# Graph sums join Strassen's scheme in two GRU gates, and three buffers are halved to make room

## The chip, the cores and the metric

The kernel runs on one core of a Trainium2 chip. A core has five engines that run side by side: TensorE (PE in the profile; its weight loads are shown apart, as PEld), VectorE (DVE), ScalarE (ACT), GpSimd (POOL) and SyncE (SP), which here only issues DMAs. The metric is the device time of one execution in microseconds (us), as the median over runs.

## What is computed

The layer works on 32 graphs of 512 nodes with 256 features each, in float32:

```python
h = relu(layernorm(x))                              # x: (32, 512, 256)
c = relu(bn1(conv1x1(h)))
x_conv = relu(bn2(conv17(c)) + h)                   # 17 taps along the nodes
s = h @ w_se.T + b_se
A = exp(-|s_n - s_m|^2) * adj
x_nmp = A @ relu(h @ w_msg.T + b_msg)               # the graph sums
gi = concat(x_conv, x_nmp) @ w_ih.T + b_ih          # (.., 768): parts r, z, n
gh = h @ w_hh.T + b_hh
r = sigmoid(gi_r + gh_r); z = sigmoid(gi_z + gh_z)
out = x + (1 - z) * tanh(gi_n + r * gh_n) + z * h
```

## The kernel before

**Layout.** Features stand on the 128 partitions (two halves of 128, the `i` or `o` of the code) and the 512 nodes of a batch along the free dimension. One batch is one graph.

**The streams.** The program is written as five Python generators, "streams": `begins` (normalise and transpose a batch), `rows` (the 1x1 convolution), `conv` (the 17-tap convolution), `graphs` (messages, the exponential, the mask, the graph sums) and `gates` (the GRU). A small planner at the end of the kernel keeps estimated times of every engine and tile. At each step it continues the stream whose clock is least among those not held, and it writes the instructions in that order, once for all. After each step `fill()` gives DVE background work: normalisation, the convolution's operands and the sums below. So the order on each engine is fixed when the kernel is built, and any edit shifts it everywhere after.

**The convolution** is done in seven groups along the nodes of all batches, with a nested scheme of 5 x 5 = 25 products a group. Its operands are made on DVE: `operands(g)` calls `fives` on h1, the stored result of the 1x1 convolution, in 6 phases for the outer operand x1 (two buffers, each about 6.6 KB a partition), and again on each x1 in 2 phases for the inner operands x2. `fives` makes the five combinations with twelve DVE instructions at the outer level. Operands are made at most a few products ahead.

**The input.** `fetch(b)` loads x of batch b into `x_sb` (two buffers). `norm` normalises it in place. From batch TURNED = 8 on `begin(b)` stores it to DRAM, reads it back in 32 x 32 blocks, transposes those on DVE and stores the result as HD[b]; it then has the input of batch b + 2 loaded. Before batch 8 TensorE transposes. In the early part a pool `prep` holds the weights in preparation; `late_pools()` closes it and opens `late` in its place, where all that the gates need stands.

**The gates.** `gates(b)` runs `unit(o)` for both output halves. Batches 1 to 30 are "fast" (FIRST_FAST = 1, PLAIN = 1): for the reset gate r and the update gate z together, the product of the weights (2 x 2 blocks: gate by input half) with the data (2 x 2 blocks: input half by node half, HALF = 256) is done with Strassen's scheme in Winograd's form: seven products of 256 columns in place of eight. `weight_sums()` makes the weights' combinations once (`wsum`), `data_sums(b)` those of the data for each batch on DVE (`tsum`: t13 of 512 elements, t2 and t4 of 256 each). `term(...)` writes one of the seven products for each of its sources. Before the change these are h (`hTb`, with `whh`) and x_conv (`xconv`, with the first half of `wih`). The third source, the graph sums (`xnb`, with the second half of `wih`), is added in the plain way, two matmuls of 512 columns a gate, by the calls

```python
yield from products(ps_r, o, 0, (2,), reset, clear=False)
yield from products(ps_z, o, 1, (2,), update, clear=False)
```

The order in a fast unit is: first r term; a copy of it to `ps_z` on ScalarE; products of the new gate of the unit before (`some_new`); three terms; the fifth product copied out (`fifth`) and added on DVE to r's and z's other half (`spread`), with further products between; the last r term, r's graph sums, `reset()` (tanh on ScalarE); the new gate's hidden products (`hidden`), where they were not written earlier; the last z term, z's graph sums, `update()`. The result `r` has two buffers, `fifth` one tile of its own.

**Loads.** SP's queue issues all loads in order, `load_sums(b, d)` those of the graph sums in halves (`xnb`, two buffers of one half each), the second pair only after the first is used. POOL's queue issues the stores.

Of the kernel before, what the change touches and what calls it, by code (L numbers as in the profile page):

```python
# [13 lines left out]
P = 128  # L14
# [17 lines left out]
G = 4  # L32
# [18 lines left out]
def kernel(  # L51
# [266 lines left out]
    def fetch(b, xs=None):  # L318
        XS[b] = front.tile([P, NT, D], F32, name="x_sb", bufs=2) if xs is None else xs
        step = NT // 2 if b == 0 else NT  # L320
        for c in range(0, NT, step):
            sp.dma_start(
                XS[b][:, c : c + step], x[b].rearrange("(c p) d -> p c d", p=P)[:, c : c + step]
            )
# [48 lines left out]
    def load_sums(b, d):  # L373
        if b < B and (b, d) not in XN:
            settle_stores()
            XN[b, d] = late.tile([P, N], F32, name="xnb", bufs=2)
            sp.dma_start(XN[b, d], ND_[b, d])
            XN_AT[b] = max(XN_AT.get(b, 0.0), done(XN[b, d]))

    fetch(0)  # L380
# [6 lines left out]
    prep_ctx = ExitStack()  # L387
    prep = pool_of(prep_ctx, "prep", 1)
# [216 lines left out]

    def phases(name, n, rv, bufs):

        t = cv.tile([P, n * RV], F32, name=name, bufs=bufs)
        return t[:, : n * rv].rearrange("p (q e) -> p q e", e=rv)

    def operands(g):

        rv = sizes(g)[3]
        h = h1[:, : Q * rv].rearrange("p (q e) -> p q e", q=Q)
        for x1 in fives(h, 6, rv, lambda: phases("x1", 6, rv, 2), again=True):
            yield None
            if x1 is not None:
                yield from fives(x1, 2, rv, lambda: phases("x2", 2, rv, 6))
# [298 lines left out]
    def convolution():  # L917
# [28 lines left out]
        for g in range(NG):  # L946
# [9 lines left out]
            for n in range(25):  # L956
# [6 lines left out]
                if late is None and len(WS) >= 25 and prep.over() <= now + 1.0:  # L963
                    late_pools()
# [47 lines left out]
    def late_pools():  # L1012
        nonlocal late, wih, whh, wsum, tsum
        prep_ctx.close()
        late = pool_of(ctx, "late", 1)
        late.born = prep.over()
        whh = late.tile([P, ND, 3 * D], F32, name="whh")
        wih = late.tile([P, 2 * ND, 3 * D], F32, name="wih")
        sp.dma_start(whh, w_hh)
        sp.dma_start(wih, w_ih)  # L1020
        wsum = late.tile([P, 2, 3, D], F32, name="wsum")
        tsum = [
            [late.tile([P, n, HALF], F32, name=f"t{k}_{j}") for j, n in enumerate((2, 1, 1))]
            for k in range(2)
        ]
# [3 lines left out]
    def weight_sums():  # L1029


        for k, w in enumerate((whh, wih)):
            a11, a12 = w[:, 0, :D], w[:, 1, :D]
            a21, a22 = w[:, 0, D : 2 * D], w[:, 1, D : 2 * D]
            s1, s2, s4 = (wsum[:, k, j, :] for j in range(3))
            dve.tensor_tensor(s1, a21, a22, op=ALU.add)
            dve.tensor_tensor(s2, s1, a11, op=ALU.subtract)
            dve.tensor_tensor(s4, a12, s2, op=ALU.subtract)
            dve.tensor_tensor(a21, a11, a21, op=ALU.subtract)
# [6 lines left out]
    def data_sums(b):  # L1046


        step = T_STEP.get(b, 0)
        if step == 6 or b >= B - PLAIN or sums_free[step > 3] != b:  # L1050
            return
        n, k = divmod(step, 2)
        if (RES if k else HB_AT).get(b, 1e9) > now:
            return
        t = XC[b] if k else HB[b]
        t13, t2, t4 = tsum[k]
        if n == 0:
            dve.tensor_tensor(
                t13, t[:, :, HALF:], t[:, 0, :].rearrange("p (h n) -> p h n", h=2),
                op=ALU.subtract,  # L1060
            )
        elif n == 1:
            dve.tensor_tensor(t2[:, 0], t[:, 1, HALF:], t13[:, 0], op=ALU.subtract)
        else:
            dve.tensor_tensor(t4[:, 0], t[:, 1, :HALF], t2[:, 0], op=ALU.subtract)
        T_STEP[b] = step + 1
        if k == 1:
            T_AT[b, n] = dve.free + 0.3
# [95 lines left out]
    def begin(b):  # L1164
# [4 lines left out]
        if b >= TURNED:  # L1169
# [19 lines left out]
            if b + 2 < B:  # L1189
                later(now + 2.0, lambda: load(b + 2))  # L1190
# [6 lines left out]
        for d in range(ND):  # L1197
            yield gps.free("ps_g")
            norm_t(b, d)
            if d == ND - 1:  # L1200
                begun, turning = b + 1, False
                if b < 2 or b >= G:
                    load(b + (G if b < 2 else 2))
            yield now
# [53 lines left out]
    def gates(b):  # L1258
# [8 lines left out]
        if not NEW:  # L1267
            load_sums(b, 0)
            load_sums(b, 1)
# [7 lines left out]
        def products(ps, o, g, ks, then=None, of=None, clear=True):  # L1277
# [4 lines left out]
            for k in ks:  # L1282
# [9 lines left out]
                if k == 2 and o == ND - 1 and g == 2:  # L1292
                    for d in range(ND):
                        later(now + 2.0, lambda d=d: load_sums(b + 1, d))
# [57 lines left out]
        if b == B - PLAIN:  # L1352
            for w, at in ((whh, w_hh), (wih, w_ih)):
                sp.dma_start(w[:, 0, D : 2 * D], at[:, 0, D : 2 * D])
        def some_new(n):
# [9 lines left out]
            while NEW and n > 0:  # L1365
                NEW.pop(0)()
                n -= 1
                if last and len(NEW) == 2:
                    for d in range(ND):
                        later(now + 0.5, lambda d=d: load_sums(NEW_B[0] + 1, d))  # L1370
# [7 lines left out]
        def unit(o):  # L1378
            r = z = None

            def reset():
                nonlocal r
                if is_last(o):
                    load_res(b, o)
                if OPEN > 1:
                    settle()
                r = late.tile([P, N], F32, name="r", bufs=2)
                act.activation(r, ps_r, AF.Tanh, bias=brz[:, o : o + 1], scale=0.5)
# [41 lines left out]
            if fast:  # L1430
# [9 lines left out]
                sources = ((whh, hT), (wih, XC[b]))  # L1440

                def term(ps, weight, data, begin=False, end=False):
                    for k, (w, t) in enumerate(sources):
                        matmul(
                            ps, weight(k, w), data(k, t),
                            start=(begin and k == 0), stop=(end and k == 1), skip_group_check=True,
# [29 lines left out]
                term(ps_r[:, lo], given(0, 0), part_of(0, lo), begin=True)  # L1476
                if UPDATED[0] < UPDATED[1]:
                    yield now + 0.5
                    if UPDATED[0] < UPDATED[1]:
                        settle()  # L1480
                ps_z = acc.tile([P, N], F32, name="ps_acc")
# [4 lines left out]
                if o == 0:  # L1486
                    for d in range(ND):
                        load_sums(b, d)
                    x_in.extend([XC[b][:, i, :] for i in range(ND)] + [XN[b, d] for d in range(ND)])
                    yield lambda: (b, 1) in T_AT  # L1490
                    yield T_AT[b, 1]
# [4 lines left out]
                fifth = late.tile([P, HALF], F32, name="fifth")  # L1496
# [15 lines left out]
                term(ps_r[:, hi], summed_w(2), part_of(1, hi))  # L1512
                yield XN_AT[b]
                yield from products(ps_r, o, 0, (2,), reset, clear=False)
# [9 lines left out]
                if o == 0:  # L1524
                    yield lambda: (b, 2) in T_AT
                    yield T_AT[b, 2]
                yield z_at
                term(ps_z[:, lo], given(1, 1), summed_t(3))
                if o == ND - 1:
                    sums_free[1] = b + 1  # L1530
                yield now
                UPDATED[1] += 1
                yield from products(ps_z, o, 1, (2,), update, clear=False)
                if o == 0:
                    load_gates(b + 1)

# [16 lines left out]
            if not fast:  # L1553
# [3 lines left out]
                if o == 0:  # L1557
# [4 lines left out]
                    x_in.extend([XC[b][:, i, :] for i in range(ND)] + [XN[b, d] for d in range(ND)])  # L1562
# [265 lines left out]
```

## Time and profile before

| what | value |
|---|---|
| median of 3 runs | 2047.43 us (2046.34 to 2051.44) |
| the profiled execution: its own time | 2048.43 us |
| its span, from the first to the last instruction | 2046.7 us |
| VectorE busy | 1440.9 us, 70% |
| ScalarE busy | 878.0 us, 43% |
| DMA | 185 GB/s on average |
| mean granted TensorE clock | 0.991 of full speed |

The numbers of the profile come from one execution and stand beside its own time. A group of the profile is written as line, engine, operation, output<-inputs, shape and count, then the busy time in us and the mean time of one in ns, then the engine's idle time just before and what ended it. Most instructions pass through helpers, so their line is the helper's (L241 for DVE and ScalarE, L259 for matmuls) and they are told apart by their tiles. A float32 matmul appears as two MATMUL instructions with two weight loads. The drawn ends of matmuls overlap the next one, so their cost is read from start to start.

### The profile page before, as it was taken

How to read it: one execution, taken by the hardware profiler on the slowest of the kernel's cores; microseconds unless marked ns; L12 is line 12 of the kernel's file. 1: busy time of each engine (PE TensorE's matmuls, PEld its weight loads, DVE VectorE, ACT ScalarE, POOL GpSimd, SP SyncE). 2: the span in 40 equal slices, each digit the busy share in tenths (PEclk: the TensorE clock that was granted, in tenths of full speed). 3: DMA queues.
4: the chain of work that ended last, by engine and by line, in shares of the span. 5: the costliest groups of instructions: out<-in, count | busy, mean ns of one | idle time of the engine just before them, and what ended most of it. 6: DMA issues, size and time to landing. Idle time of an engine off the chain costs nothing. (4 is left out here: it accounts for less than half of the span.)

```text
span 2046.7 us, 27748 instructions
## 1 busy us (share of the span) xinstructions
PE 2002.3 (98%) x9347; PEld 1382.9 (68%) x9347; DVE 1440.9 (70%) x2686; ACT 878.0 (43%) x1755; POOL 448.2 (22%) x578
## 2 busy tenths in 40 slices
PE   8999999999999999999999999999999999999998
PEld 4777666666776657776677675667766676675664
DVE  5779787978887368885787774678975678763433
ACT  5554563344534353433453334444244533334221
POOL 2100021231221232122232212241212311113232
PEclk9999999999999999999999999999999999999999
DMA  7455587798897779887887788797985978746564
GB/s 260 171 183 176 204 255 216 185 257 201 224 211 208 175 176 228 191 211 173 203 213 180 187 201 184 165 199 214 221 204 136 200 193 180 161 102 125 88 98 42
DMA packets 581230, 378.75 MB, mean 185 GB/s; under 512 B 457648, under 2 KB 475344, under 8 KB 579952
## 3 DMA queue, kind: packets, MB, share of 16 engines
q1 hardware_dynamic: 419616, 279.02, 49.3%
q0 software_dynamic: 153184, 84.70, 24.0%
q10 hardware_dynamic: 8288, 13.24, 1.8%
q8 instruction: 75, 1.23, 0.2%
q14 instruction: 67, 0.55, 0.1%
HBM read 278.81 MB, written 114.56 MB: 192 GB/s over the span
## 5 line engine op out<-in xcount | busy, mean ns | idle before, releaser
L228 POOL DMA_DIRECT2D out_dram<-o_sb x252 | 275.9, 1728 | 612.7 <-DVE o_sb L241 540.5
L259 PE MATMUL ps_acc<-xnb,wih 128*128 128x512 f32 (+1 forms) x772 | 366.5, 591 | 0.8 <-DVE ps_acc L241 0.7
L259 PEld LDWEIGHTS ps_c<-xd,w 128*128 128x128 f32 x2304 | 285.8, 190 | 50.3 <-ACT ps_c L241 32.4
L259 PEld LDWEIGHTS ps_c<-x,w 128*128 128x128 f32 x2032 | 260.3, 194 | 65.0 <-issue 39.2
L259 PE MATMUL ps_c<-xd,w 128*128 128x135 f32 (+1 forms) x2304 | 290.9, 279 | 1.3 <-ACT ps_c L241 1.1
L259 PE MATMUL ps_c<-x,w 128*128 128x135 f32 (+2 forms) x2032 | 268.6, 281 | 7.2 <-ACT z L241 5.1
L259 PE MATMUL ps_g<-at,msg 128*128 128x512 f32 x512 | 227.4, 593 | 2.1 <-DVE shift L241 1.2
L259 PE MATMUL ps_acc<-hTb,whh 128*128 128x512 f32 (+2 forms) x532 | 213.1, 497 | 5.6 <-ACT r L241 5.6
L259 PE MATMUL ps_acc<-xconv,wih 128*128 128x512 f32 (+2 forms) x532 | 209.1, 495 | 1.8 <-DVE ps_acc L241 1.0
L259 PEld LDWEIGHTS ps_acc<-xnb,wih 128*128 128x128 f32 x772 | 140.4, 190 | 95.8 <-issue 85.8
L241 DVE TENSOR_TENSOR ps_acc<-ps_acc,fifth 128x256 f32<-128x256 f32 x120 | 51.2, 427 | 204.6 <-PE ps_acc L259 188.1
L259 PEld LDWEIGHTS ps_g<-at,msg 128*128 128x128 f32 x512 | 95.6, 190 | 110.4 <-issue 103.1
L259 PEld LDWEIGHTS ps_acc<-hTb,whh 128*128 128x128 f32 x532 | 94.9, 190 | 68.6 <-issue 51.6
L241 DVE SCALAR_TENSOR_TENSOR x<-x,x 128x544 f32<-128x544 f32 (+5 forms) x161 | 137.8, 856 | 3.8
L241 DVE TENSOR_TENSOR msg<-ps_g,bmsg 128x256 f32<-128x256 f32 x128 | 53.3, 418 | 119.9 <-PE ps_g L259 119.7
L259 PEld LDWEIGHTS ps_acc<-xconv,wih 128*128 128x128 f32 x532 | 98.0, 190 | 50.0 <-issue 38.8
L241 DVE TENSOR_TENSOR x<-x 128x272 f32<-128x272 f32 (+5 forms) x280 | 127.8, 497 | 0.4
L259 PE MATMUL ps_g<-wmsg,hTg 128*128 128x259 f32 x496 | 125.1, 382 | 0.0
L259 PE MATMUL ps_acc<-t,wsum 128*128 128x256 f32 x480 | 123.5, 379 | 0.8 <-DVE wsum L241 0.8
L259 PE MATMUL ps_g<-hT,w 128*128 128x512 f32 (+8 forms) x296 | 120.5, 553 | 3.5 <-DMA hT<-hd 3.4
L241 ACT ACTIVATE h<-ps_g,bn_shift,bn_scale 128x252 f32<-128x252 f32 (+8 forms) x212 | 86.6, 483 | 62.9 <-PE ps_g L259 60.1
L259 PEld LDWEIGHTS ps_acc<-t,wsum 128*128 128x128 f32 x480 | 90.0, 190 | 31.3 <-issue 18.7
(147 smaller groups left out, 2984.0 us busy)
## 6 DMA issues: line engine op xcount, KB each, us to landing
w<-wd SPq DMA_DIRECT2D x414, 256.0 KB, 3.8
m_sb<-in_adj_dram SPq DMA_DIRECT2D x384, 64.0 KB, 3.9
hT<-hd SPq DMA_DIRECT2D x33, 512.0 KB, 4.5
hd<-hT POOLq DMA_DIRECT2D x32, 512.0 KB, 5.6
hTb<-hd SPq DMA_DIRECT2D x32, 512.0 KB, 5.4
xnb<-nd SPq DMA_DIRECT2D x64, 256.0 KB, 3.5
out_dram<-o_sb POOLq DMA_DIRECT2D x252, 64.0 KB, 4.7
hTg<-hd SPq DMA_DIRECT2D x31, 512.0 KB, 4.2
```

The lines of the kernel that those rows point to most:

```text
L228: self.engine.dma_start(dst, src, **more)
L241: getattr(self.engine, op)(*tiles, **more)
L259: nc.tensor.matmul(ps, lhsT, rhs, **more)
```

## The change

1. The graph sums become a third source of `term`. `wsum` and `tsum` get a third part; `weight_sums` and `data_sums` make it; the plain products of the graph sums in r and z go. `data_sums` now walks two lists, one for h and x_conv, one for the graph sums, a step of each at a call. `reset()` and `update()` follow the last term directly.
2. The graph sums of a batch are one tile of both halves with two buffers, so that they can be loaded a batch ahead. The first r term is split: its part with the graph sums waits for their load.
3. The fifth product is put into the first half of `r`, which is therefore allotted earlier (`make_r`).
4. The outer operand x1 has one buffer from group 1 on: `fives_alone` makes each of the five combinations from the one before, in place. In group 0 the old function is used, with buffers from two pools.
5. The input has one buffer. Odd batches below 8 use one in `prep`; from batch 8 on the load of b + 1 starts when b is turned. `late_pools()` also waits for eight batches begun and 25 operands.

```diff
     def fetch(b, xs=None):
-        XS[b] = front.tile([P, NT, D], F32, name="x_sb", bufs=2) if xs is None else xs
+        if xs is None:
+            pool_ = prep if b % 2 and b < TURNED else front
+            xs = pool_.tile([P, NT, D], F32, name="x_sb" if pool_ is front else "x_odd", bufs=1)
+        XS[b] = xs
...
+            XN[b] = late.tile([P, ND, N], F32, name="xnb", bufs=2)
+            for d in range(ND):
+                sp.dma_start(XN[b][:, d, :], ND_[b, d])
...
+        for steps in (
+            ((minus, 3, 1),),
+            ((minus, 2, 0), (less2, None, 3), (minus, None, 1)),
+            ((minus, 3, 1), (less2, None, 4), (minus, None, 2)),
+            ((minus, 2, 1), (less2, None, 3), (minus, None, 2)),
+            ((minus, 3, 2), (less2, 1, None)),
+        ):
+            for k, (op, a, b) in enumerate(steps):
+                op(a, b)
+                yield t if k == len(steps) - 1 else None
...
-        for x1 in fives(h, 6, rv, lambda: phases("x1", 6, rv, 2), again=True):
+        if g == 0:
+            more = iter([cv, prep] * 2)
+            firsts = fives(h, 6, rv, lambda: x1_of(next(more), rv), again=True)
+        else:
+            firsts = fives_alone(h, 6, rv, x1_of(cv, rv))
+        for x1 in firsts:
...
-                if late is None and len(WS) >= 25 and prep.over() <= now + 1.0:
+                if late is None and len(WS) >= 25 and len(X2) >= 25 and begun >= TURNED and prep.over() <= now + 1.0:
                     late_pools()
...
-            if b + 2 < B:
-                later(now + 2.0, lambda: load(b + 2))
+            if b + 1 < B:
+                later(now + 0.3, lambda: load(b + 1))
...
-                sources = ((whh, hT), (wih, XC[b]))
+                if o == 0:
+                    load_sums(b)
+                sources = ((whh, hT), (wih[:, :ND], XC[b]), (wih[:, ND:], XN[b]))
...
                 ps_r = acc.tile([P, N], F32, name="ps_acc")
-                term(ps_r[:, lo], given(0, 0), part_of(0, lo), begin=True)
+                term(ps_r[:, lo], given(0, 0), part_of(0, lo), begin=True, of=(0, 1))
...
+                if o == 0:
+                    yield XN_AT[b]
+                term(ps_r[:, lo], given(0, 0), part_of(0, lo), of=(2,))
...
-                fifth = late.tile([P, HALF], F32, name="fifth")
+                make_r()
+                fifth = r[:, :HALF]
                 act.activation(fifth, ps_r[:, hi], AF.Copy)
...
-                term(ps_r[:, hi], summed_w(2), part_of(1, hi))
-                yield XN_AT[b]
-                yield from products(ps_r, o, 0, (2,), reset, clear=False)
+                term(ps_r[:, hi], summed_w(2), part_of(1, hi), end=True)
+                reset()
+                yield now
...
-                term(ps_z[:, lo], given(1, 1), summed_t(3))
+                term(ps_z[:, lo], given(1, 1), summed_t(3), end=True)
                 if o == ND - 1:
                     sums_free[1] = b + 1
+                UPDATED[1] += 1
+                update()
                 yield now
-                UPDATED[1] += 1
-                yield from products(ps_z, o, 1, (2,), update, clear=False)
```

In `fives_alone` an operation that reads phase 3 or later is written twice, once for five phases and once for the sixth; `minus` subtracts, `less2` takes twice its first from its second, and None stands for the buffer itself. The load of the sums moves from the end of a batch's new-gate products (there for the next batch) to the same place for the batch after that.

## The prediction

> **What bounds the kernel now.** I read the page's busy times first, then the same by stage, then what TensorE waits for, then TensorE's order of work where nothing else runs. The busy times:
>
> ```profile
> PE 2002.3 (98%) x9347; PEld 1382.9 (68%) x9347; DVE 1440.9 (70%) x2686; ACT 878.0 (43%) x1755; POOL 448.2 (22%) x578
> ```
>
> TensorE (PE) is busy for all but 44.4 us of the 2046.7 us span. By stage (us; busy and count of each engine; granted clock; DMA share; GB/s):
>
> ```profile
> 0.00:250.00 250.00, 233.85 (x1347) 178.31 (x1348) 184.81 (x401) 134.91 (x298) 28.85 (x64) 0.95 0.56 194
> 250.00:600.00 350.00, 337.82 (x1707) 238.98 (x1706) 292.60 (x545) 162.66 (x328) 76.87 (x109) 1.00 0.85 225
> 600.00:1855.00 1255.00, 1246.39 (x5719) 857.22 (x5719) 893.17 (x1619) 527.06 (x1046) 286.50 (x350) 1.00 0.80 187
> 1855.00:2046.70 191.70, 184.25 (x579) 108.34 (x577) 70.38 (x123) 53.41 (x84) 56.00 (x55) 0.99 0.55 88
> ```
>
> PE's idle time is 16.2, 12.2, 8.6 and 7.5 us in the four stages. From 600 us on it hardly waits, though VectorE (DVE) runs at 71% there; from 800 to 900 us DVE was at 89.65% and PE idle for nothing. Only from 250 to 600 us (DVE 83.6%) does PE lose a little. The longest waits:
>
> ```profile
> PE ps_acc L259 <- ACT r L241: 5.6, 12, 1.6
> PE ps_c L259 <- ACT z L241: 5.4, 3, 4.3
> PE ps_g L259 <- DMA hT<-hd: 3.4, 6, 1.0
> ```
>
> None is worth more than 6 us. So the time is PE's columns, and a change is first counted in columns. What a column costs is read where only the gates run, from start to start, since the drawn durations overlap (start, us, instruction, count):
>
> ```profile
> 1904.46 1.03 PE L259 MATMUL ps_acc<-t,wsum 128*128 128x256 f32 x4
> 1905.33 0.59 PE L259 MATMUL ps_acc<-hTb,whh 128*128 128x256 f32 x2
> 1905.76 0.59 PE L259 MATMUL ps_acc<-xconv,wih 128*128 128x256 f32 x2
> 1906.19 1.03 PE L259 MATMUL ps_acc<-t,wsum 128*128 128x256 f32 x4
> 1907.05 1.88 PE L259 MATMUL ps_acc<-xnb,wih 128*128 128x512 f32 x4
> ...
> 1910.50 1.88 PE L259 MATMUL ps_acc<-xnb,wih 128*128 128x512 f32 x4
> 1912.21 1.88 PE L259 MATMUL ps_acc<-hTb,whh 128*128 128x512 f32 x4
> 1913.93 0.38 PE L259 MATMUL ps_acc<-t,whh 128*128 128x256 f32 x1
> ```
>
> From 1904.46 to 1907.05 stand 12 instructions of 256 columns: 0.2158 us each. From 1910.50 to 1913.93 stand 8 of 512: 0.4288 us each. The code writes two matmuls where the trace has four, so one matmul is two instructions: 0.432 and 0.858 us. The costs follow columns; 256-column weight loads (190 ns) hide under them.
>
> **What the Trainium skill says.** "TensorE: Matmul & The Clock Gate", Back-to-back issue gap, puts the warm gap at N/2.4 + 2.5 ns. One instruction here takes twice the columns' share (429 ns for 512, where the formula gives 216), and the trace decides; the small fixed part agrees (two of 256 cost 431.6 ns, 3 more than one of 512). "Perfetto Trace Analysis", Identifying the Most-Contended Engine, warns that matmul busy time is no measure of the roofline; here it serves only to show that PE has no holes, and weight loads stand at 68%. "VectorE: DVE Perf Modes", The TRN2 errata, prices an f32 two-operand add at (N+151)/0.96 ns: 1584 ns at 1360+10 elements, where the row below has 1578. The same trace-analysis page calls ScalarE and VectorE strict FIFO (Tensor Engine Instruction), which matters for the fifth product below.
>
> **The change, part by part.**
>
> *PE.* The reset and update gates of batches 1 to 30, two output halves each, are 60 units. Now each unit spends four matmuls of 512 columns on the graph sums (two for each gate): 60 x 4 x 2 = 480 instructions. (The group of xnb has 764 of 512 columns: 60 units x 12, with the new gate's, plus 44 in the two plain batches.) They go: 480 x 0.4288 = 205.8 us. Each of the seven Strassen terms gains one matmul of 256: 60 x 7 x 2 = 840 instructions, 840 x 0.2158 = 181.3 us. Net -24.5 us. Weight loads rise by 360 x 190 ns = 68 us on an engine at 68%, under matmuls that are longer than a load.
>
> *DVE, graph sums.* Three more operations per fast batch, like those on xconv: 673 + 415 + 415 = 1503 ns, x30 = 45.1 us. Four more weight sums at 0.42 us, once: 1.7 us.
>
> *DVE, outer operand in one buffer.* Rows concerned:
>
> ```profile
> L241 DVE TENSOR_TENSOR x<-h 128x1360 f32<-128x1360 f32 x12 | 18.8, 1568 | 4.1 <-ACT h L241 4.1
> L241 DVE TENSOR_TENSOR x<-h 128x1370 f32<-128x1370 f32 x6 | 9.5, 1578 | 12.1 <-ACT h L241 12.1
> L241 DVE TENSOR_TENSOR x<-h 128x272 f32<-128x272 f32 x12 | 5.2, 433 | 0.0
> ```
>
> Counted from both functions, a group now has six wide steps and three split in 5+1 phases; after, six and six: +3 x 1.57 + 3 x 0.43 = 6.0 us, in six groups 36 us. Group 0 keeps the old form.
>
> DVE thus gains 45.1 + 1.7 + 36 = 83 us (1441 to about 1524, 75% of a shorter span). It counts only where PE comes to wait. No run shows that share, so I bound it, stage by stage:
> - 0 to 250 us: nothing is added. The later room also waits for eight batches begun (133 us in the trace) and 25 operands; group 1's first operand starts at 230 us, the room opens at 239 us. 0.
> - 250 to 600: about 1.7 groups (10), four or five batches of sums (7), weight sums (1.7): 19 us, DVE from 84 to 89%. Bounds: -6 (half its idle time vanishes in the new order) and +19. If idle grows as DVE's slack shrinks, 12.2 x (16.4/11 - 1) = 6; if with its work, 0.8. I take 4.
> - 600 to 1855: about 55 us more, 71 to 76%. Bounds -4 and +55; by slack 8.6 x (28.8/24.4 - 1) = 1.6. I take 1.5, as DVE at 90% cost nothing there.
> - the end, gates alone: the reset gate's sum is followed by fewer columns. Between it and the new-gate products that need its result PE had 1.72 (graph sums) + 1.72 (hidden) + 0.86 + 1.72 + 0.86 = 6.9 us, and will have 1.72 + 1.3 + 1.3 = 4.3 us (2.6 where the hidden products come first), for tanh 0.69, two handovers of 0.2, DVE 0.69, and 1.1 us of new sums that may stand ahead: 2.9 us plus what else DVE has queued. Bounds 0 and 1 us a batch; six batches; I take 2 in all.
>
> *Other edits.* The fifth product in r's tile: tanh of r must now wait until DVE has read the fifth for the update gate. In the trace that read ended over 1.5 us after its product in 28 of 60 units, 29 us beyond in total; ScalarE (43% busy) stands still meanwhile, with its conversions for the convolution behind it. The order of work is written with these waits known, and other streams fill PE: 0, bounds 0 and 5. Nothing is saved by it either.
> The input in one buffer: from batch 9 on a load starts when the one before is turned. Serial then: load 5.4, statistics 2.3, rstd and shift 1.9, ScalarE 2.4, store 5.5, eight reload issues 3.9 and landing 2.8, two transposes 1.4: 25.6 us. The trace has 24 such batches from 177.7 to 1601.8 us: 59 us each. Hidden by graph work; without that cover each us over costs 24. 0.
> The graph sums loaded together and a batch ahead on SP's queue: the same 64 issues; the trace stores each at least 100 us before its gates in the steady part. 0.
>
> Sum: -24.5 + 4 + 1.5 + 2 = -17. On the profiled execution: span 2046.7 - 17 = 2029.7, with 1.7 around it 2031.4; the median of runs is 1.0 below that execution's 2048.43, so 2047.4 - 17 = **2030.4**; I say 2030.
>
> **The rivals.**
> *Nothing is lost* (2023): all added DVE work is hidden, 2047.4 - 24.5. For it: bulk windows with DVE at 90% and no idle PE. Against: 12.2 us idle at 84% from 250 to 600 us.
> *DVE eats the gain* (2047): 24.5 of the 83 us, 30%, come through to PE. Speaks for it: both additions fall in the convolution's stretches, where some 25 us slices already show DVE at 97 to 98%. Against: PE was not idle in those after 600 us.
> *DVE becomes the bound* (2064, slower): in those stretches operands come late, the convolution stalls, the gates find no finished batch, and half the addition is exposed: 2047.4 - 24.5 + 41.6 = 2064.5. It decides from (24.5 + 6)/83 = 37% on.
> *The single input buffer becomes the bound*: only if its 25.6 us more than doubled to 59; at 60.5 it would eat 24 x 1.5 = 36 us. The chain of waits gives hT<-hd half a per cent.
>
> **How the numbers follow.** Likeliest, a small loss (2025 to 2036): 0.64. Nothing lost, below 2025: 0.18. A larger loss, up to 2041: 0.07. Between 2041 and 2054: 0.06. Slower, either bound: 0.05. A change under 0.3% (6 us) can't be told from none, so faster is 0.64 + 0.18 + 0.07 = 0.89. Range 2020 to 2039: the low end needs 3 us of idle time regained, the high end 16 us of the 83 exposed.
>
> **What the profile would show.** 284 xnb instructions of 512 columns, and 840 more of 256; PE busy near 1978; DVE near 1524; PE idle near 50; at the end a batch every 28.5 to 29.3 us in place of 29.7. Wrong would be idle PE of over 60 us, with waits on DVE's x or w, or on hT<-hd.

## The result, and the profile after

The kernel after takes **2038.90 us** (median of 5 runs, 2034.87 to 2041.01), the kernel before beside it 2049.05. The ratio is 0.9951 with a 95% interval of 0.9937 to 0.9964: 7.4 to 12.9 us faster, where 17 were forecast. 2038.9 lies at the very end of the range given (2020 to 2039).

The profiled execution of after took 2034.87 us with a span of 2033.1, against 2048.43 and 2046.7. So the profile shows 13.6 us of gain, the medians 10.2: the profiled execution of after was the fastest of its five, the one of before stood 0.6 below its median. The busy times on the page of after:

```profile
PE 1979.4 (97%) x9707; PEld 1448.2 (71%) x9707; DVE 1512.4 (74%) x2816; ACT 876.4 (43%) x1755; POOL 450.9 (22%) x578
```

PE's busy time falls by 22.9 us and its idle time rises from 44.4 to 53.7: -22.9 + 9.3 = -13.6. Where the idle time is, the same stages show (us; busy and count of each engine; granted clock; DMA share; GB/s):

```profile
0.00:250.00 250.00, 234.39 (x1356) 177.12 (x1357) 188.85 (x405) 135.09 (x299) 29.39 (x65) 0.97 0.57 199
250.00:600.00 350.00, 339.93 (x1767) 249.45 (x1765) 304.03 (x568) 162.45 (x327) 84.15 (x113) 1.00 0.86 224
600.00:1855.00 1255.00, 1236.41 (x6001) 912.20 (x6001) 949.19 (x1720) 525.02 (x1050) 281.20 (x345) 1.00 0.80 187
1855.00:2033.10 178.10, 168.69 (x587) 109.39 (x585) 70.31 (x126) 53.81 (x80) 56.13 (x58) 0.99 0.58 91
```

PE's idle time by stage is now 15.6, 10.1, 18.6 and 9.4 us (before 16.2, 12.2, 8.6, 7.5). All the growth that matters is in the long middle stage: **+10.0 us from 600 to 1855**, where 1.5 were forecast. There is no single wait behind it. PE's longest waits over the whole span (us in total, times, longest):

```profile
PE ps_acc L259 <- DVE ps_acc L241: 5.9, 8, 1.5
PE ps_g L259 <- DMA hT<-hd: 3.5, 5, 1.8
PE ps_c L259 <- ACT ps_c L241: 3.5, 7, 0.9
PE ps_c L259 <- ACT n L241: 3.4, 3, 2.1
PE ps_acc L259 <- ACT ps_acc L241: 2.8, 1, 2.8
```

None is longer than before's longest (4.3 us). They are mostly other kinds of waits: the first had 2.3 us before, the last three under 1.8 each. Of the waits that the prediction had named as the sign of an error, those on DVE's x or w are not among them, and hT<-hd is where it was: 3.4 us before, 3.5 now.

The columns went as forecast. PE's order at the end, from start to start (start, us, instruction, count, idle time before):

```profile
1921.98 1.46 PE L259 MATMUL ps_acc<-t,wsum 128*128 128x256 f32 x6
1923.28 0.59 PE L259 MATMUL ps_acc<-hTb,whh 128*128 128x256 f32 x2
1923.71 0.59 PE L259 MATMUL ps_acc<-xconv,wih 128*128 128x256 f32 x2
1924.14 0.59 PE L259 MATMUL ps_acc<-xnb,wih 128*128 128x256 f32 x2
1924.57 1.46 PE L259 MATMUL ps_acc<-t,wsum 128*128 128x256 f32 x6
1925.87 1.88 PE L259 MATMUL ps_acc<-xnb,wih 128*128 128x512 f32 x4
...
1934.95 1.55 PE L259 MATMUL ps_acc<-xnb,wih 128*128 128x512 f32 x3 [0.31 <-DVE ps_acc L241]
```

From 1921.98 to 1925.87 stand 18 instructions of 256 columns, 0.216 us each as before; three sources stand in each term; only the new gate's xnb instructions are of 512. The last line is the stall that the prediction expected at the end. DVE's order just ahead of it shows why:

```profile
1932.08 0.68 DVE L241 TENSOR_TENSOR t<-xnb 128x512 f32<-128x512 f32 x1
1932.68 0.70 DVE L241 STREAM_TRANSPOSE o_sb<-r 128x512 f32<-128x512 f32 x1
1933.31 0.65 DVE L241 TENSOR_TENSOR t<-xconv 128x512 f32<-128x512 f32 x1
1933.88 0.41 DVE L241 TENSOR_TENSOR t<-xnb,t 128x256 f32<-128x256 f32 x1
1934.21 0.69 DVE L241 SCALAR_TENSOR_TENSOR ps_acc<-r,ps_acc 128x512 f32<-128x512 f32 x1
```

The reset product (last line) stands behind two of the new sums on xnb, with a transpose and a sum on xconv between them, and PE's xnb products stand behind it. Such waits make up 2.6 us in the end stage (us in total, times, longest); the end stage of before has none of them:

```profile
PE ps_acc L259 <- DVE ps_acc L241: 2.6, 5, 1.5
```

A batch at the end takes 29.0 us (loads of hTb start at 1914.7, 1943.7 and 1972.7), where 29.7 were read before.

### The profile page after: what moved, and what is told of

It is laid out like the page before. It is cut to its first block, busy times and chain, and to the rows that moved or that the text cites. A ratio compares the mean times of both kernels' runs of the same rounds, so it can differ in the third digit from the quotient of the medians.

```text
span 2033.1 us, 28623 instructions
## 1 busy us (share of the span) xinstructions
PE 1979.4 (97%) x9707; PEld 1448.2 (71%) x9707; DVE 1512.4 (74%) x2816; ACT 876.4 (43%) x1755; POOL 450.9 (22%) x578
## 3 DMA queue, kind: packets, MB, share of 16 engines
q0 software_dynamic: 153184, 84.70, 24.5%
## 5 line engine op out<-in xcount | busy, mean ns | idle before, releaser
L259 PE MATMUL ps_acc<-xnb,wih 128*128 128x512 f32 (+2 forms) x532 | 209.3, 495 | 3.7 <-DVE ps_acc L241 3.4
L241 DVE TENSOR_TENSOR ps_acc<-ps_acc,r 128x256 f32<-128x256 f32 x120 | 51.6, 430 | 212.0 <-PE ps_acc L259 200.1
L259 PE MATMUL ps_acc<-t,wsum 128*128 128x256 f32 x720 | 177.1, 382 | 5.3 <-ACT ps_acc L241 2.8
L259 PEld LDWEIGHTS ps_acc<-t,wsum 128*128 128x128 f32 x720 | 135.7, 191 | 41.8 <-issue 17.8
L259 PEld LDWEIGHTS ps_acc<-xnb,wih 128*128 128x128 f32 x532 | 96.2, 190 | 44.9 <-issue 29.2
L259 PE MATMUL ps_acc<-t,wih 128*128 128x256 f32 x480 | 123.2, 379 | 0.0
```

What stands on the lines that cost most here:

```text
L241: getattr(self.engine, op)(*tiles, **more)
L259: nc.tensor.matmul(ps, lhsT, rhs, **more)
```

## The experiments

The question was where some 7 of 17 us went. Three theories were held in turn: the added work on DVE; the gates' stream coming to stand where a batch's convolution isn't finished (with PE faster, the planner's pace for it is out of date); one of the edits that free memory. Against each stood the same rival: the order of work. The planner writes one order for the whole kernel, so an edit can give another order, with its own waits. Names that begin with b_ are edits of the kernel before, those with a_ edits of the kernel after.

### The parts of the change by themselves

**b_narrow**: the columns alone. The graph sums of r and z in the fast batches are computed on 448 of 512 columns: 480 instructions x 64 columns = 25.6 us less on PE. Nothing else is edited, but the planner's order changes: PE's instructions follow each other as before for the first 1916 of 9347 (371 us), then differently.

```diff
+                    n = 448 if fast and k == 2 and g < 2 else N
                     matmul(
-                        ps, w[:, at + i, cols(o, g)], hT[:, i, :] if k == 0 else x_in[2 * k - 2 + i],
+                        ps[:, :n], w[:, at + i, cols(o, g)], (hT[:, i, :] if k == 0 else x_in[2 * k - 2 + i])[:, :n],
```

> The kernel before, with the graph sums of the fast reset and update gates taken on 448 of the 512 columns (64 nodes get no graph sums there): 480 instructions of 448 in place of 512 columns, 480 x 64/1194 us per thousand = 25.7 us less TensorE work, and nothing else edited. Theory A (saved columns come through one for one): ratio about 0.9875, 24 to 27 us less, PE idle near 45 us. Theory B (about half of any saving in the gates is lost again to other waits, whatever DVE does): 11 to 16 us less, PE idle 53 us or more.

Measured: 2030.55 us, ratio 0.9908 (0.9894 to 0.9922). Of 25.6 us, 18.5 come through, which lies between the two theories (24 to 27 and 11 to 16). DVE's work is as it was:

```profile
PE 1978.9 (97%) x9347; PEld 1384.5 (68%) x9347; DVE 1440.2 (71%) x2686; ACT 878.0 (43%) x1755; POOL 449.4 (22%) x578
```

In its middle stage PE is idle about as long as in the kernel after:

```profile
600.00:1855.00 1255.00, 1237.65 (x5741) 862.49 (x5740) 896.21 (x1626) 526.42 (x1048) 288.77 (x350) 1.00 0.80 187
```

PE is idle for 17.3 us there (8.6 before, 18.6 after), although no instruction was added to DVE, ScalarE or a queue. So idle time of this size can arise without any added DVE work.

**b_outer**: point 4 of the change alone (one outer buffer, `fives_alone`), which adds DVE work and takes nothing from PE.

```diff
-        for x1 in fives(h, 6, rv, lambda: phases("x1", 6, rv, 2), again=True):
...
+            firsts = fives_alone(h, 6, rv, x1_of(cv, rv))
+        for x1 in firsts:
```

> The kernel before with the one outer buffer alone (the in-place combinations from group 1 on): DVE +36 us, PE unchanged. If added DVE work is what costs (theory DVE): 3 to 8 us slower, as its share of 83 us. If DVE work is hidden and the loss lies elsewhere: within 2 us.

Measured: 2047.97 us, ratio 0.9992 (0.9982 to 1.0001). DVE's busy time is 1473.6 us, 32.7 more, and the kernel is no slower:

```profile
PE 1999.9 (98%) x9347; PEld 1381.4 (68%) x9347; DVE 1473.6 (72%) x2722; ACT 877.8 (43%) x1755; POOL 452.3 (22%) x578
```

**b_input**: point 5 alone (one input buffer).

```diff
...
-            if b + 2 < B:
-                later(now + 2.0, lambda: load(b + 2))
+            if b + 1 < B:
+                later(now + 0.3, lambda: load(b + 1))
...
```

> The kernel before with the one input buffer alone: no engine has more work. Theory DVE: within 2 us. Theory buffers (the loads that start later make the convolution late): 5 to 12 us slower, with PE waits on hT<-hd or x_sb.

Measured: 2059.80 us, ratio 1.0044 (1.0029 to 1.0060): by the ratio 9 us slower, by itself, as theory buffers expected; but the waits that grew are not those on the input that it named. From 600 to 1855 us PE waits for ScalarE's part of the convolution (us in total, times, longest):

```profile
PE ps_c L259 <- ACT z L241: 6.6, 5, 3.6
PE ps_c L259 <- ACT ps_c L241: 4.2, 6, 2.2
PE ps_g L259 <- DMA hT<-hd: 2.3, 2, 1.6
```

hT<-hd, which a late input would show, has 2.3 us, less than before's 3.4 in that stage. The TensorE clock takes part too: its granted share is 0.989 on average over the six executions, against 0.993 over the executions of before. By that estimate (the time multiplied by 1 minus the clock) some 8 us more are withheld here. Whether the 9 us belong to the buffer or to the order that came with it was left for the last runs.

### Taking the added DVE work out of the kernel after

**a_nosum_few**: the kernel after, with the data sums of xnb made for the first fast batch alone, and the outer operand's five in-place combinations cut to a shorter list of steps (both leave work out of the result).

```diff
+            if k == 2 and b > FIRST_FAST:
+                T_STEP[b, source] = step + 1
+                T_AT[b, n, source] = now
+                continue
...
-            ((minus, 2, 0), (less2, None, 3), (minus, None, 1)),
...
+            ((minus, 2, 0), (less2, None, 1)),
...
```

> The changed kernel without its added DVE work: the data sums of the graph sums are made for batch 1 alone and used for all, and the outer combinations are wrong ones with the old count of wide and split instructions. DVE near 1435 us, all buffers single as in the change. Theory DVE: the whole saving of 24.5 us appears, ratio 0.987 to 0.989, PE idle 42 to 47 us. Theory buffers: it stays near the changed kernel, ratio 0.993 to 0.996, PE idle over 50 us.

Measured: 2047.59 us, ratio 0.9993 (0.9983 to 1.0003). DVE is back to 1442.9 us busy, and the kernel is 9 us slower than the kernel after, so taking the added DVE work out gains nothing here. Nor does PE wait longer:

```profile
PE 1986.4 (97%) x9707; PEld 1457.3 (71%) x9707; DVE 1442.9 (71%) x2693; ACT 878.8 (43%) x1755; POOL 449.8 (22%) x578
```

With a span of 2040.7 us its idle time is 54.3 us in all, 53.7 in the kernel after. What grew is PE's busy time, by 7.0 us with the same number of instructions: this trace stands at half clock for 50 us, that of the kernel after for 30, and over all executions the mean granted clock is 0.988 against 0.993. The order is another one as well; what in it brings the half-clock windows is not isolated.

### The order of work

Four edits change nothing but the planner's constants: where the gates' stream starts, and the handover time LAG that the planner assumes.

```diff
-        "gates": (all_gates(), 31.25 * PER, 1.8),
+        "gates": (all_gates(), 31.25 * PER, 1.7),
```

> The kernel before with one planner number changed: the gates' clock starts at 1.7 in place of 1.8. Every engine has the same work; only the order shifts. Theory order (the order before is one with unusually few waits from 600 to 1855 us, 12 us, and almost any edit draws one with 13 to 26): 3 to 12 us slower, waits there 15 us or more. Theory DVE (what the change lost is due to its added DVE work): within 2 us, waits there near 12 us.

> The changed kernel with the gates' clock at 1.7 in place of 1.8. Theory order: somewhere between 6 us faster and 6 us slower than the changed kernel, its waits from 600 to 1855 us anywhere from 12 to 30 us (22.5 in the changed kernel). Theory DVE: within 2 us of it, waits of 20 to 25 us.

```diff
-    LAG = 0.17
+    LAG = 0.18
```

> The kernel before with another planner number changed: the assumed lag after a result, 0.17 to 0.18 us. Theory order: 3 to 12 us slower, waits from 600 to 1855 us of 15 us or more. Theory DVE: within 2 us, waits near 12 us.

> The changed kernel with the assumed lag at 0.18 us. Theory order: between 6 us faster and 6 us slower than the changed kernel, waits from 600 to 1855 us from 12 to 30 us. Theory DVE: within 2 us, waits of 20 to 25 us.

Measured: with the new LAG the kernel before takes 2049.15 (ratio 1.0004), the kernel after 2039.47 (0.9959). These two are no test of the order, since the edit leaves it: in b_lag all instructions of PE, DVE and ScalarE follow each other as in before, in a_lag those of PE and ScalarE as in after. So not every edit shifts the order, and a repeated order repeats its time. The start of the gates' stream does shift it: before 2055.41 (1.0022, 1.0008 to 1.0035; as slow as theory order expected, though PE's idle time from 600 to 1855 us is 11.9 us and not 15 or more), after **2065.09** (1.0082, 1.0055 to 1.0110), 26 us above the kernel after with the same instructions in another order, far outside the 6 us to either side that were expected.

In a_shift the gates stand at batches where the convolution's result comes late: the load of `xconv` starts 58.6 us after that of `hTb` for batch 22 and 39.9 for batch 27 (21.3 and 12.0 in the kernel after, at most 2.3 before). That suggested a remedy: set the gates' pace to PE's new speed, or start them later.

```diff
-        "gates": (all_gates(), 31.25 * PER, 1.8),
+        "gates": (all_gates(), 30.4 * PER, 1.8),
```

> The changed kernel with the gates' pace set to their new cost: 30.4 in place of 31.25 (a fast batch takes 28.4 us of TensorE in place of 29.3). Theory pace (cheaper gates run ahead of the convolution on the planner's old pace, stand still at batches 22 and 27 for want of a finished convolution, and leave TensorE without cover): the stops of 21 and 12 us vanish or fall below 5 us, waits from 600 to 1855 us fall from 22.5 to 12-17 us, 4 to 10 us faster than the changed kernel, ratio 0.990 to 0.993. Theory DVE: stops may vanish, waits stay at 20 us or more, ratio 0.994 to 0.996. Theory order (any edit draws anew): waits anywhere from 13 to 26.

> The changed kernel with the gates' clock starting at 1.9 in place of 1.8, the other way to keep them behind the convolution. Theory pace: shorter stops (below 12 us), waits of 13 to 19 us from 600 to 1855 us, 2 to 8 us faster than the changed kernel. Theory DVE: waits of 20 us or more, within 2 us of it. Theory order: either sign.

> The kernel with the graph sums of the fast reset and update gates on 448 columns, which lost 7 us of its 25.6, now with the pace at 30.4. Theory pace: its stops of 25 and 12 us vanish and nearly the whole saving comes through, ratio 0.987 to 0.989. Theories DVE and order: stays near 0.991.

> The changed kernel without its added DVE work (data sums of the graph sums made for batch 1 alone, wrong outer combinations of the old cost), which came out at 0.9993, with the pace at 30.4. Theory pace: stops of 36 and 12 us vanish, ratio 0.988 to 0.992. Theory order: anywhere from 0.990 to 1.000. Beside a_pace it shows what the added DVE work costs when no stop disturbs: by theory DVE 5 us or more between the two, by theory pace under 4.

Measured: a_pace 2052.38 (1.0019, 1.0007 to 1.0031), a_start (start 1.9) 2050.21 (1.0002), b_narrow_pace 2029.98 (0.9912), a_nosum_few_pace 2042.30 (0.9969). In a_pace and a_start no `xconv` load comes more than 2 us late, so these stops are gone, and both are slower than the kernel after by 11 us and more, where 2 to 10 us faster was expected. b_narrow_pace is rid of its stops too (at most 2.3 us late) and is no faster than b_narrow. The stops were a sign, not the loss; this theory falls. In a_start the waits of the middle stage have become waits for DVE (us in total, times, longest):

```profile
PE ps_acc L259 <- DVE ps_acc L241: 10.9, 10, 2.1
PE ps_g L259 <- DVE at L241: 6.3, 2, 5.0
```

One comparison had been foreseen as the price of the added DVE work: a_pace beside a_nosum_few_pace, 5 us or more by theory DVE, under 4 by theory pace. It came out at 10.1 us, and in the traces most of the difference is PE's idle time, 66.1 us against 57.1 (spans 2055.2 and 2044.8):

```profile
PE 1989.1 (97%) x9707; PEld 1452.7 (71%) x9707; DVE 1510.6 (74%) x2816; ACT 873.2 (42%) x1755; POOL 450.2 (22%) x578
PE 1987.7 (97%) x9707; PEld 1456.3 (71%) x9707; DVE 1444.0 (71%) x2693; ACT 875.0 (43%) x1755; POOL 451.7 (22%) x578
```

At the old pace taking the same work out made the kernel 8.7 us slower. The two pairs contradict each other, and in both PE's order differs too. So a price of several us for the added DVE work is neither shown nor excluded.

### The fifth product

Another view, of what ScalarE waits for, set the kernels apart: in those with the fifth product in r's tile, ScalarE stands under the tanh of r until DVE has read the fifth, 5.4 us in the kernel after, 26.9 in a_nosum_few, 33.7 in a_shift; with a tile of its own, not at all. Four kernels tested it.

```diff
...
-                fifth = late.tile([P, HALF], F32, name="fifth")
+                make_r()
+                fifth = r[:, :HALF]
```

> The kernel before with the fifth product in r's tile and nothing else. Theory 'fifth' (ScalarE stands still under the tanh of r until VectorE has read the fifth, with the convolution's conversions queued behind it): ScalarE waits 10 to 30 us in all for that read (0 before), TensorE's waits in 600 to 1855 us rise from 11.6 to 17 to 22 us, the time by 5 to 10 us, to 2054 to 2059. Theory 'order' (fewer columns per unit leave less to put between dependent steps, whatever the tile): nothing of that is in this kernel, within 3 us of before, waits 11 to 14 us.

In the three others the tanh is issued when DVE is due to have read the fifth:

```diff
-                act.activation(r, ps_r, AF.Tanh, bias=brz[:, o : o + 1], scale=0.5)
+                if at > now:
+                    later(at, tanh)
+                else:
+                    tanh()
...
-                reset()
+                reset(z_at - LAG)
```

> The kernel after, with the tanh of r issued on ScalarE only when VectorE is due to have read the fifth, so that other ScalarE work goes ahead of it. Theory 'fifth': ScalarE's wait for that read falls from 5.4 us to under 1, TensorE's waits in 600 to 1855 us from 22.5 to 15 to 19, time 2033 to 2036. Theory 'order': the waits stay at 20 to 26 us, time 2037 to 2042 or worse.

> The same edit in the kernel that makes the data sums for the first fast batch alone and fewer steps of the outer operand (it leaves that work out), where ScalarE's wait for the read was 26.9 us in 10 places. Theory 'fifth': that wait falls to under 3 us, TensorE's waits in 600 to 1855 us from 26.0 to 15 to 19, time from 2047.6 to 2037 to 2041. Theory 'order': waits 22 us or more, time above 2043.

> The kernel after with the same edit, and the outer operand's combinations written with other factors, so that ten steps are wide and four are split where twelve and six were: 24 us less on VectorE, the same results. Theory 'fifth': 2030 to 2036, at or below the kernel after. Theory 'order': any value from 2035 to 2050, with waits of 20 us or more in 600 to 1855 us. Theory 'VectorE' (already contradicted): clearly below a_tanh.

Measured: b_fifth 2049.89 (1.0004, 0.9992 to 1.0015), a_tanh 2038.39 (0.9957), a_nosum_few_tanh 2047.74 (0.9996), a_cheap_tanh 2064.94 (1.0081, 1.0068 to 1.0095). b_fifth has the wait that was expected, from 600 to 1855 us:

```profile
ACT r L241 <- DVE ps_acc L241: 16.3, 5, 4.3
```

and it costs nothing that can be told: PE's order is that of before, instruction for instruction, its idle time in that stage is 10.8 us (8.6 before), and the time is the same. This is the clean test. The remedy did less than it was meant to: in a_tanh the wait fell from 5.4 to 4.1 us only, in a_nosum_few_tanh from 26.9 to 15.1, and neither time moved. This theory falls too; the "0" that the prediction gave this edit stands. a_cheap_tanh does the outer operand with 24 us less on DVE and is 26 us slower than the kernel after, which no theory had expected: another order with long waits, 17.8 us of them for `xconv` (16.9 in one wait near the end), and a mean granted clock of 0.986.

### Are the parts additive?

**b_narrow_input** is b_narrow with the input buffer, **b_narrow_all** with the outer buffer and the fifth as well: all of the change but the third source of Strassen's scheme, in whose place the 448 columns stand. Their edits are those shown above.

> The kernel before with the graph sums of the reset and update gates on 448 of 512 columns (the graph sums of 64 nodes are left out of these gates) and one input buffer. Theory 'input' (the single buffer costs its 9 us whatever else is changed): 2038 to 2042, where b_narrow has 2030.5; TensorE's waits in 600 to 1855 us from 21 to 27 or more. Theory 'order' (each edit gives another order of work, whose cost is its own): no sum is to be expected, within 4 us of 2030.5 or off it by any amount to either side; a value of 2034 or less contradicts 'input'.

> The same with the outer buffer and the fifth product in r's tile added: all edits of the change but the third source of Strassen's scheme, whose saving stands in by 448 columns (the same part is left out). Theory 'input': 2037 to 2041, as b_narrow_input, since outer buffer and fifth cost nothing alone. Theory 'order': over 4 us off b_narrow_input in either direction.

Measured: 2032.17 (0.9915, 0.9902 to 0.9929) and 2031.83 (0.9907, 0.9893 to 0.9922). The input buffer that costs 9 us alone costs 1.6 us here, within what such runs tell apart. So the 9 us are not a fixed price of the buffer but came with that order, and in these two orders the edits that free memory take nothing from the gain that can be told. Theory input falls; b_narrow_all, 0.3 us from b_narrow_input, is not over 4 us off it either, as theory order had it.

### PE's idle time from 600 to 1855 us, by what PE was about to write

This table is worked out from the instruction starts in each trace: the idle time ahead of each matmul, put to its output. `ps_acc` is the gates, `ps_c` the convolution and some of the exponential, `ps_g` the graphs and the 1x1 convolution. The last column is an estimate from another source: the time multiplied by 1 minus the granted clock, averaged over all executions of a kernel.

| kernel | ps_acc | ps_c | ps_g | sum | median us | withheld by the clock, us |
|---|---|---|---|---|---|---|
| before | 4.3 | 0.9 | 3.4 | 8.6 | 2049.0 | 14.1 |
| b_outer | 0.5 | 6.3 | 3.5 | 10.3 | 2048.0 | 18.0 |
| b_input | 0.9 | 13.1 | 2.3 | 16.2 | 2059.8 | 22.6 |
| b_narrow | 4.1 | 6.4 | 6.8 | 17.3 | 2030.6 | 17.1 |
| b_narrow_all | 5.4 | 5.6 | 6.7 | 17.7 | 2031.8 | 19.1 |
| after | 9.3 | 7.9 | 1.4 | 18.6 | 2038.9 | 15.1 |
| a_tanh | 11.0 | 6.2 | 1.7 | 18.9 | 2038.4 | 16.3 |
| a_nosum_few | 8.5 | 8.3 | 4.2 | 20.9 | 2047.6 | 25.1 |
| a_pace | 16.3 | 10.3 | 4.7 | 31.3 | 2052.4 | 19.8 |
| a_shift | 14.4 | 5.6 | 12.1 | 32.1 | 2065.1 | 31.5 |

Three things can be read from it. With the columns saved on 448 of 512, four orders (b_narrow_input with 16.4 and b_narrow_pace with 15.4 are not in the table) have sums of 15.4 to 17.7. Without the saving, the order of before has 8.6 (8.9 in b_lag and 10.8 in b_fifth, which have the same PE order), b_outer 10.3, b_shift 11.9, and b_input 16.2. Single traces of one PE order differ by about 3 us: after has 18.6, a_lag 21.8. Second, the gates' own waits are 6.7 us and above in every kernel that has the graph sums as a third source (6.7 in a_nosum_few_pace), 5.4 and below in every one that hasn't, whether DVE was relieved or not. Third, part of the differences goes with the clock and not with the waits: b_input against before, a_nosum_few against after and a_shift against after differ by 8.5, 10 and 16 us in the last column, where their times differ by 9, 9 and 26.

No kernel here that computes the whole result is clearly better than the kernel after: a_tanh's 2038.39 can't be told from it.

## Why the prediction was right and wrong

**The columns: right.** -24.5 us were forecast. From the trace of before to that of after PE has 480 instructions of 512 columns less (2060 to 1580) and 840 of 256 more (1680 to 2520), which is -24.5 at the measured prices. There are 284 xnb instructions of 512 columns, as forecast; PE's busy time is 1979.4 (forecast 1978). It fell by 22.9 us, although the trace of after also loses 4.2 us less at half clock (15.0 against 19.2). So by an estimate from these figures some 6 us of stalls (24.5 + 4.2 - 22.9) are drawn as busy, and the idle times understate the waiting.

**The added DVE work: right in size.** The rows of the kernel after, for the sums on xnb:

```profile
L241 DVE TENSOR_TENSOR t<-xnb 128x512 f32<-128x512 f32 x30 | 20.5, 684 | 2.4 <-DMA xnb<-nd 2.4
L241 DVE TENSOR_TENSOR t<-xnb,t 128x256 f32<-128x256 f32 x60 | 25.1, 418 | 2.5 <-PE ps_acc L259 2.3
```

20.5 + 25.1 = 45.6 us, 45.1 forecast; the outer buffer adds 36.9 us in b_outer if all durations are summed, 36 forecast. In all DVE's summed durations rise by 86.1 us (1581.2 to 1667.3), 83 forecast. Its busy time rises by 71.5, because the drawn times of instructions that follow at once overlap and the busy time counts the overlap once.

**Stage by stage.** Forecast 0, +4, +1.5 and +2 us of idle time; measured -0.6, -2.1, +10.0 and +1.9. The end is right in size and in cause, waits for DVE's reset product, which stands behind new sums. In the second stage, from which the evidence for a loss by DVE had been taken, there was none.

**The step that failed is the middle stage: "600 to 1855 ... I take 1.5, as DVE at 90% cost nothing there".** That stage lost 10.0. The observation agrees with b_outer, where 33 us more DVE work left the time as it was. The error was to let only DVE's added work make waits: b_narrow removes columns and adds nothing, and PE's idle time in that stage doubles, by 8.7 us. A saving on a PE that is 98% busy was worth 72% there (18.5 of 25.6 us), and not 100% less a DVE term. Of the 7 us lost some 3 are the clock's, by the table's estimate (17.1 against 14.1).

Whether the missing columns bring the waits, or the order that comes with them, is not separated. Three more orders with the same columns have them, but two of these contain the input edit, which has 16.2 us without the saving. One explanation fits and is argued only: before, PE ran almost without a hole because its 1246 us of work stood in front of what the other engines had to finish, and with less of it the same convolution and the same loads are met sooner, at many places by a little. The rival is theory order: before is a favourable order, and almost any change of order loses some of it. b_input agrees with it, b_outer and b_shift (10.3 and 11.9) less so. To tell them apart one would have to take the columns away and keep before's order.

**The rest of the gap.** The kernel after is 7.1 us above b_narrow_all, which differs from it in the third source, with its sums and loads, and in the order. The profiled executions are 5.0 apart (2034.87 and 2029.87), and all of that is idle time: 1.2 and 1.1 us in the first two stages, 0.9 in the middle stage, 2.2 at the end (9.4 us against 7.2). In the middle stage the gates wait 3.9 us longer and the convolution 2.3, but the graphs 5.3 less. Only the end's part is the mechanism that the prediction priced: fewer PE columns between a result of DVE and the product that needs it, with sums ahead of it on DVE. The plain graph sums, 3.4 us of PE work a unit that waited for nothing in Strassen's scheme, used to stand in these gaps; in the kernel after each term waits on its sums. That the gates' own waits are longer in every kernel with the third source fits this for the middle stage too, but it was not isolated: a kernel with the third source and other work in the gaps was not built. It stays open.

**In numbers.** On the profiled executions the error is +8.5 us in the middle stage, -6.7 in the two before it, -0.1 at the end, and 1.6 in the busy time: 3.3 us in all (13.6 against 17). So errors of opposite sign cancel, and that the total still lies within the range is luck in part: the range had been widened for exposed DVE work, not for what happened. The other 3.4 us lie between that execution and the median. No trace shows the slower runs, so they are not explained. The clock is not the reason for the miss as a whole: it withholds 14.1 us from before and 15.1 from after.

**The rivals.** "Nothing is lost" fell: 2023 was not reached, and b_narrow loses 7 us with no DVE work added. "DVE becomes the bound" fell: the kernel after is faster than before. "DVE eats the gain" is not supported as a whole, since b_outer adds 33 us to DVE and is no slower, and a_nosum_few takes 70 away and isn't faster; but a_nosum_few_pace is 10.1 us faster than a_pace, and in the middle stage of a_pace and a_start PE's largest waits in total are those for DVE's ps_acc (10.1 and 10.9 us). A part of the loss by this mechanism can't be excluded, since orders with the same instructions range from 2038 to 2065 us. "The single input buffer becomes the bound" fell in its mechanism, hT<-hd; the 9 us that the edit costs alone came with its order, in part as time at half clock, and vanished in another. What was missing is a rival for the order itself: the prediction took "other streams fill PE" for granted, and a_shift shows that the same work can cost 26 us more, slower than before.

## What to carry to other kernels

A saving on an engine that is busy 98% of the time need not be worth its full price: take the columns away alone first, in whatever form, and see what comes through. Where one program plans the whole order, an edit's price includes the order that comes with it, here between 0 and 26 us, so a part that costs 9 us alone may cost nothing in company; give the range room for it, and compare parts in company and not only alone. And a long wait on an engine with time to spare (ScalarE, 16 us) says nothing until the bound engine is seen to wait behind it. Before a difference is put down to waits, look at the granted clock of all executions: the traces of after and a_nosum_few have the same PE work and nearly the same idle time, and are 7.6 us apart.

## What the runs showed of the hardware

A short wait can cost twice. In the kernel after PE waits 2.11 us at 1410.5 for ScalarE's n, and its granted clock is then half for 6.8 us (columns as above: us; busy and count of PE, PEld, DVE, ACT, POOL; clock; DMA share; GB/s):

```profile
1405.70:1412.50 6.80, 4.83 (x31) 3.82 (x29) 6.70 (x11) 1.53 (x6) 0.00 (x0) 1.00 0.77 300
1412.60:1419.40 6.80, 6.75 (x26) 4.74 (x27) 6.80 (x11) 5.22 (x7) 4.37 (x4) 0.50 0.82 41
1419.50:1426.30 6.80, 6.33 (x39) 5.34 (x39) 5.16 (x9) 4.69 (x10) 0.00 (x0) 1.00 0.48 160
```

The only other such window from 600 us to the last batch, 3.4 us from 1614.0, follows the other long wait, 2.83 us:

```profile
1613.77 2.78 PE L259 MATMUL ps_acc<-t,wsum 128*128 128x256 f32 x6 [2.83 <-ACT ps_acc L241]
1616.34 1.06 PE L259 MATMUL ps_acc<-hTb,whh 128*128 128x256 f32 x2
```

Six instructions take 2.57 us there instead of 1.29. The Trainium skill ("TensorE: Matmul & The Clock Gate", HAM oscillation — how this bites in real kernels) puts the danger at idle gaps above about 3.4 us. In this case shorter ones are enough. The 20 traces together, from 250 us to 30 us before the last matmul, were counted, a window being put to a wait if it begins during the wait or within 1.7 us after it. Of the waits of PE of 1 to 2 us 12 of 146 have a half-clock window, of those of 2 to 3 us 26 of 38, of those above 3 us 22 of 25. Of the 78 windows 18 follow no wait of 1 us, as in before at 1233.5 us, so what sets one off isn't settled here.

A window of 3.4 us takes 1.7 us where PE has work throughout. Until their last batches the traces of before, after and b_input lose 17.1, 13.7 and 22.2 us in such windows. That this is time lost shows in the 166 executions of before beside the experiments: the 18 with a granted clock of 0.991 or less take 2053.1 us on average, the 21 with 0.995 or more 2047.1.
